# Where the softmax sums are added, and when finished units are written back, in a two-layer graph kernel on one core

## The chip, the cores and the metric

The kernel runs on one core of one Trainium2 chip. The core has five engines with instruction streams of their own: TensorE (PE in the profile) for matrix products and transposes, VectorE (DVE), ScalarE (ACT), GpSimd (POOL) and SyncE (SP), which here starts most transfers. TensorE writes its results to PSUM, a small memory from which VectorE and ScalarE read. The metric is the device time of one execution in microseconds (us), as the median of several runs.

## The reference

Two layers, each followed by a residual sum and a layer norm. The first is a graph convolution with batch norm, the second a masked attention with 4 heads of 64 over 2048 nodes, for each of 8 batches of 256 features. The change touches the second alone.

```python
# layer 0: x is (8, 2048, 256), adj is (2048, 2048)
x = _layernorm(x + _L0_gnn_ref(x, adj, W1, b1, g1, be1, W2, b2, g2, be2))
# layer 1
qkv = h @ W                                   # W: (256, 768)
q, k, v = ...                                 # 4 heads of 64
mask = jnp.where(adj == 0, -jnp.inf, 0.0)
scores = jnp.einsum('bhid,bhjd->bhij', q, k) / np.sqrt(HEAD_DIM) + mask
attn = jax.nn.softmax(scores, axis=-1)
out = jnp.einsum('bhij,bhjd->bhid', attn, v)  # heads side by side: (8, 2048, 256)
x = _layernorm(x + out)
```

## The kernel before

Layer 0 ends at about 1510 us of the profiled span. The attention then works on 64 units, one for each batch (8), pair of heads (HP = 2) and block of 512 query columns (NCH = 4), so 8 units to a batch. A unit has 16 steps, one for each tile of 128 keys. Scores of both heads are computed transposed (keys on partitions), masked by adding a large negative number, raised to the exponential without subtracting a maximum, multiplied by v, and divided by their sum at the end. (A second path with maxima runs only if a sum leaves a safe range.)

One step, in the four functions that every step calls:

```python
def scores(g):                     # PE: "S" in the prediction
    st = ps_s.tile([P, 2, CH], F32, name="st")          # ps_s: 2 buffers
    for h in range(2):
        hs = slice(h * HD, (h + 1) * HD)
        for r in range(2):
            nc.tensor.matmul(st[r * HD : (r + 1) * HD, h, :],
                kt[hs, j * P + r * HD : j * P + (r + 1) * HD], qt[hs, cols], start=True, stop=True)

def mask_scores(g, st):            # DVE
    p = probs[g] = ap_.tile([P, 2, CH], F32, name="prob", bufs=13)
    nc.vector.scalar_tensor_tensor(p, mask[...], MASKED, st, op0=ALU.mult, op1=ALU.add)

def exps(g):                       # ACT
    nc.scalar.activation(probs[g], probs[g], AF.Exp)

def weigh(g):                      # PE: "W"
    if j == 0:
        outs[u] = ps_o.tile([P, 2, CH], F32, name="out_ps")   # ps_o: 1 buffer
    ...                            # 4 matmuls into outs[u], summed over the 16 steps

def add_up(g):                     # GpSimd: sums over the key tiles
    if j == 1:
        accs[u] = ap_.tile([P, 2, CH], F32, name="acc")
        nc.gpsimd.tensor_add(accs[u], probs[g - 1], probs[g])
    elif 1 < j < NT - PE_SUM:      # PE_SUM = 3, NT = 16: 12 adds to a unit
        nc.gpsimd.tensor_add(accs[u], accs[u], probs[g])
```

What follows when a unit is done. All small PSUM tiles are called `pm` and share a pool of two buffers (`ps_m`, bufs=2): those of the sums, of the transposes and of the projections.

```python
def finish_out(u):                 # in step 15, right behind weigh
    ots[u] = ap_.tile([P, CH], F32, name="ot")
    nc.scalar.copy(ots[u], outs[u][:, 0, :])
    nc.vector.tensor_add(ots[u], outs.pop(u)[:, 1, :], ots[u])

def finish_sums(u):                # PE: the last PE_SUM tiles and acc, over partitions
    pm = ps_m.tile([P, BR], F32, name="pm")
    parts = [probs.pop(g) for g in range((u + 1) * NT - PE_SUM, (u + 1) * NT)]
    parts.append(accs.pop(u))
    for n, part in enumerate(parts):
        for h in range(2):
            for q in range(2):
                nc.tensor.matmul(pm[...], ones[:, :32], part[:, h, q * BR : (q + 1) * BR],
                                 start=(n == 0), stop=(n == len(parts) - 1))
    ...
    nc.scalar.copy(sts[u], pm)     # the tile "sm"

def finish_turn_sums(u):           # PE: 2 transposes; DVE: copy out, reciprocal
    pq = ps_m.tile([P, 2, P], F32, name="pm")
    for i in range(2):
        nc.tensor.transpose(pq[:, i, :], sm[:, i * P : (i + 1) * P], ident)
    nc.vector.tensor_copy(sums_all[:, u]..., pq...)
    nc.vector.reciprocal(sts[u], sums_all[:, u])

def finish_turn(u):                # PE: 4 transposes of "ot"
    pm = pms[u] = ps_m.tile([P, TPC, P], F32, name="pm")
    for i in range(TPC):
        nc.tensor.transpose(pm[:, i, :], ot[:, i * P : (i + 1) * P], ident)

def finish(u, half):               # DVE: 4 small products added to x1
    ...
```

Beside this, each batch's input is prepared while the batch before it is worked on, by functions of `Layer1Input`: `load` (DMA), `bn` (ACT), `norm` (PE transposes; DVE sum and layer norm statistics), `root` (GpSimd, four small instructions), `apply` (ACT), `turn` (PE transposes of x1 into `pm`, ACT copies them out) and `project` (PE products for q, k or v into `pm`; ACT or DVE copies them out). Finished rows get their last layer norm by `emit_stats` (DVE), `root` and `emit` (ACT, then DMA out).

```python
def apply(self, b, c, half):       # ACT: 2 instructions on x1
    self.ln[b, c].apply(range(IT * half, IT * (half + 1)))

def turn(self, b, c, half):
    pm = self.psum.tile([P, ND, BR], F32, name="pm")
    ...                            # 4 transposes
    nc.scalar.copy(self.x1t[b][:, :, r0 : r0 + BR], pm)

def emit_stats(self, b, c):
    ln = self.ln[b, c] = LayerNorm(self.pool, self.x1[b, c])
    ln.stats(range(TPC))           # 4 BN_STATS, 4 aggregates
```

All that stands beside the steps is put into a table by unit and step, and the order of the loop is the order of the instructions on PE, DVE, ACT and GpSimd:

```python
LEAD = 3
for u in range(NU - 1):
    b, hp, c = units[u]
    at_step(u + 1, 0, finish_sums, u)
    at_step(u + 1, 3, finish_turn_sums, u)
    at_step(u + 1, 3, finish_turn, u)
    at_step(u + 1, 3, finish, u, 0)
    at_step(u + 1, 4, finish, u, 1)
    if hp == HP - 1:
        j = 6 if c == 2 else 12
        at_step(u + 1, j, inp.emit_stats, b, c)
        at_step(u + 1, j + 2, inp.root, b, c)
        for half in range(2):
            at_step(u + 1, j + 5 + half, inp.emit, b, c, half)
# (cut: the table of the next batch's input; it is in the diff)

for g in range(NU * NT):
    u, j = divmod(g, NT)
    ahead = g + LEAD < NU * NT
    if ahead:
        st = scores(g + LEAD)
    if j == NT - 1:
        weigh(g)
        finish_out(u)
    if ahead:
        mask_scores(g + LEAD, st)
        exps(g + LEAD)
    for f, args in side.get((u, j), ()):
        f(*args)
    if j < NT - 1:
        weigh(g)
    add_up(g)
```

Of the kernel before, what the change touches and what calls it, by code (L numbers as in the profile page):

```python
# [26 lines left out]
def tile_gcn_then_masked_attention(  # L27
# [22 lines left out]
    NT = N // P  # L50
# [4 lines left out]
    NCH = N // CH  # L55
    TPC = CH // P
# [186 lines left out]
    IT = BR // P  # L243
    NU = B * HP * NCH
# [37 lines left out]
    class Layer1Input:  # L282
# [54 lines left out]
            r0 = c * CH + half * BR  # L337
            nc.scalar.copy(self.x1t[b][:, :, r0 : r0 + BR], pm)  # L338

        def emit_stats(self, b, c):  # L340
            ln = self.ln[b, c] = LayerNorm(self.pool, self.x1[b, c])
            ln.stats(range(TPC))

        def emit(self, b, c, half):
            self.apply(b, c, half)
# [46 lines left out]
    def attention():  # L392


        with tc.tile_pool(name="attn", bufs=2) as ap_, tc.tile_pool(
# [4 lines left out]
            inp = Layer1Input(ap_, ps_m, NCH + 3)  # L400
            units = [(b, hp, c) for b in range(B) for hp in range(HP) for c in range(NCH)]
            probs, accs, outs, ots, sts, pms = {}, {}, {}, {}, {}, {}

            PE_SUM = 3

            def scores(g):
                u, j = divmod(g, NT)
# [15 lines left out]
            def mask_scores(g, st):  # L423
                j, cols = g % NT, units[g // NT][2] * CH
                cols = slice(cols, cols + CH)
                p = probs[g] = ap_.tile([P, 2, CH], F32, name="prob", bufs=13)
                nc.vector.scalar_tensor_tensor(  # L427
                    p, mask[:, j, cols][:, None, :].to_broadcast([P, 2, CH]), MASKED, st,
                    op0=ALU.mult, op1=ALU.add,
                )  # L430

            def exps(g):
                nc.scalar.activation(probs[g], probs[g], AF.Exp)  # L433
# [16 lines left out]
            def add_up(g):  # L450
                u, j = divmod(g, NT)
                if j == 1:
                    accs[u] = ap_.tile([P, 2, CH], F32, name="acc")
                    nc.gpsimd.tensor_add(accs[u], probs[g - 1], probs[g])  # L454
                elif 1 < j < NT - PE_SUM:
                    nc.gpsimd.tensor_add(accs[u], accs[u], probs[g])  # L456

            def finish_out(u):
# [4 lines left out]
            def finish_sums(u):  # L463

                pm = ps_m.tile([P, BR], F32, name="pm")
                parts = [probs.pop(g) for g in range((u + 1) * NT - PE_SUM, (u + 1) * NT)]
                parts.append(accs.pop(u))
                for n, part in enumerate(parts):
                    for h in range(2):
                        for q in range(2):  # L470
                            r0 = 32 * (2 * h + q)
                            nc.tensor.matmul(  # L472
                                pm[r0 : r0 + 32, :], ones[:, :32],
                                part[:, h, q * BR : (q + 1) * BR],
                                start=(n == 0), stop=(n == len(parts) - 1),
                            )
                for g in range(u * NT, (u + 1) * NT - PE_SUM):
                    del probs[g]
                sts[u] = ap_.tile([P, BR], F32, name="sm")
                nc.scalar.copy(sts[u], pm)  # L480

            def finish_turn_sums(u):
                sm = sts.pop(u)
# [4 lines that stand above are left out]
                nc.vector.tensor_copy(  # L488
                    sums_all[:, u].rearrange("p (q i) h -> p i h q", q=2),
                    pq.rearrange("p i (h q r) -> p i h q r", h=2, q=2)[:, :, :, :, 0],  # L490
                )
                sts[u] = ap_.tile([P, TPC, 2], F32, name="ri")
                nc.vector.reciprocal(sts[u], sums_all[:, u])

            def finish_turn(u):
                pm = pms[u] = ps_m.tile([P, TPC, P], F32, name="pm")
                ot = ots.pop(u)
                for i in range(TPC):
                    nc.tensor.transpose(pm[:, i, :], ot[:, i * P : (i + 1) * P], ident)  # L499

            def finish(u, half):
                b, hp, c = units[u]
                for i in range(IT * half, IT * (half + 1)):
                    t = inp.x1[b, c][:, i, :]
                    for h in range(2):
                        z = t[:, hp * P + h * HD : hp * P + (h + 1) * HD]
                        nc.vector.scalar_tensor_tensor(
                            z, pms[u][:, i, h * HD : (h + 1) * HD], sts[u][:, i, h : h + 1], z,
                            op0=ALU.mult, op1=ALU.add,
                        )  # L510
# [4 lines left out]
            side = {}  # L515

            def at_step(u, j, f, *args):
                u, j = u + j // NT, j % NT
                side.setdefault((u, j), []).append((f, args))

            per_b = HP * NCH
            for u in range(NU - 1):
                b, hp, c = units[u]
                at_step(u + 1, 0, finish_sums, u)
                at_step(u + 1, 3, finish_turn_sums, u)
                at_step(u + 1, 3, finish_turn, u)
                at_step(u + 1, 3, finish, u, 0)
                at_step(u + 1, 4, finish, u, 1)
                if hp == HP - 1:
                    j = 6 if c == 2 else 12  # L530
                    at_step(u + 1, j, inp.emit_stats, b, c)
                    at_step(u + 1, j + 2, inp.root, b, c)
                    for half in range(2):
                        at_step(u + 1, j + 5 + half, inp.emit, b, c, half)
            for b in range(B):
                u0 = b * per_b
                for c in range(NCH):

                    for n, w in enumerate((1, 2, 0)):
                        at_step(u0 + c, (6, 9, 12)[n], inp.project, b, 1, c, w)  # L540
                    if b + 1 == B:
                        continue

                    late = 3 * (c == NCH - 1)
                    u = u0 + 3 + c
                    at_step(u - 1, 15 + late, inp.load, b + 1, c)
                    at_step(u, 2 + late, inp.bn, b + 1, c)
                    for half in range(2):
                        at_step(u, 6 + 3 * half + late, inp.norm, b + 1, c, half)
                    at_step(u, 11 + late, inp.root, b + 1, c)  # L550
                    for half in range(2):
                        at_step(u, 13 + half + (4 if late else 0), inp.apply, b + 1, c, half)
                    for half in range(2):
                        at_step(u + 1, 4 if late else 1, inp.turn, b + 1, c, half)
                    for n, w in enumerate((1, 2, 0)):
                        at_step(u + 1, (8, 10, 13)[n] if late else (6, 9, 12)[n],
                                inp.project, b + 1, 0, c, w)

            for c in range(NCH):
                inp.load(0, c)  # L560
# [11 lines left out]
            with tc.manual_schedule(engines=IN_ORDER):  # L572
                for g in range(LEAD):
                    mask_scores(g, scores(g))
                    exps(g)
# [13 lines that stand above are left out]
                    if j < NT - 1:  # L589
                        weigh(g)  # L590
                    add_up(g)
                u = NU - 1
                b, _, c = units[u]
                finish_sums(u)
                finish_turn_sums(u)
                finish_turn(u)
                for half in range(2):
                    finish(u, half)
                inp.emit_stats(b, c)
                inp.root(b, c)  # L600
                for half in range(2):
                    inp.emit(b, c, half)

    def attention_with_maxima():

        with tc.tile_pool(name="full", bufs=2) as ap_, tc.tile_pool(
# [8 lines left out]
            inp = Layer1Input(ap_, ps_m, NCH)  # L615
            for b in range(B):
# [51 lines left out]
                                z, po, sm, z, op0=ALU.mult, op1=ALU.add  # L668
                            )
                for c in range(NCH):  # L670
                    inp.emit_stats(b, c)
                    inp.root(b, c)
                    for half in range(2):
                        inp.emit(b, c, half)
# [66 lines left out]
```

## Time and profile before

| | before |
|---|---|
| median time | 4025.23 us (4021.12 to 4027.15, 3 runs) |
| span of the profiled run | 4024.4 us |
| PE busy | 3814.2 us, 95% |
| POOL busy | 1965.4 us, 49% (before the attention it does next to nothing) |
| DVE busy | 1938.5 us, 48% |
| ACT busy | 1634.9 us, 41% |
| one GpSimd add of 128x1024 | 2365 ns |
| one DVE mask of 128x1024 | 1219 ns |
| one ACT exponential of 128x1024 | 1056 ns |
| granted PE clock, 1600 to 3990 us | 1.00 |

The shares are those of the whole span. The attention takes the last 2500 us or so, and what the change is worth is read there. In the views of the profile each line has a start in us from the span's start, a duration, an engine, a line of the kernel, the operation, what it writes and reads, and how many instructions are put together; a bracket tells how long the engine sat idle before it, and what ended that. The matmuls of PE are pipelined, so their starts tell more than their durations. A wait line has the engine, the line and tile that waited, what it waited for, and then us in total, times, and the longest wait. One matmul of the program in this number format stands as two records in the profile.

### The profile page before, as it was taken

How to read it: one execution, taken by the hardware profiler on the slowest of the kernel's cores; microseconds unless marked ns; L12 is line 12 of the kernel's file. 1: busy time of each engine (PE TensorE's matmuls, PEld its weight loads, DVE VectorE, ACT ScalarE, POOL GpSimd, SP SyncE). 2: the span in 40 equal slices, each digit the busy share in tenths (PEclk: the TensorE clock that was granted, in tenths of full speed). 3: DMA queues.
4: the chain of work that ended last, by engine and by line, in shares of the span. 5: the costliest groups of instructions: out<-in, count | busy, mean ns of one | idle time of the engine just before them, and what ended most of it. 6: DMA issues, size and time to landing. Idle time of an engine off the chain costs nothing.

```text
span 4024.4 us, 57339 instructions
## 1 busy us (share of the span) xinstructions
PE 3814.2 (95%) x24226; PEld 1580.8 (39%) x24226; DVE 1938.5 (48%) x2874; ACT 1634.9 (41%) x2005; POOL 1965.4 (49%) x1103
## 2 busy tenths in 40 slices
PE   3599999999997998999999999999999999999997
PEld 3244444444443443333333333333333333333332
DVE  6411111111112443666666666666666666666665
ACT  6000000000001434555555556556555555555554
POOL 0000000000000003778778777777787877877887
PEclk7799999999998998999999999999999999999998
DMA  5110110111003761001001001001001001000000
GB/s 209 65 53 29 45 52 34 50 53 52 32 31 131 233 205 64 5 13 38 12 17 38 12 17 38 12 17 38 12 12 43 12 12 43 12 12 24 10 1 23
DMA packets 77229, 181.80 MB, mean 45 GB/s; under 512 B 6176, under 2 KB 55840, under 8 KB 66592
## 3 DMA queue, kind: packets, MB, share of 16 engines
q1 hardware_dynamic: 67600, 123.49, 9.3%
q0 software_dynamic: 9360, 54.53, 3.3%
q8 instruction: 192, 3.15, 0.3%
q14 instruction: 77, 0.63, 0.1%
HBM read 106.70 MB, written 71.30 MB: 44 GB/s over the span
## 4 chain that ended last, share of the span: by engine, by line
PE 86%; ACT 4%; DVE 3%; issue 1%; POOL 1%; DMA 1%; SPq 0%; ACTq 0%; DVEq 0%; POOLq 0%
PE pa L183 22%; PE out_ps L445 20%; PE st L415 19%; PE pm L363 6%; PE py L229 6%; PE ph L195 5%; PE pm L375 3%; ACT prob L433 2%; ACT x L277 2%; PE pm L472 2%; DVE prob L427 2%; POOL acc L456 1%; PE pm L312 1%; PE pm L499 1%; PE pm L332 1%
## 5 line engine op out<-in xcount | busy, mean ns | idle before, releaser
L456 POOL TENSOR_TENSOR acc<-acc,prob 128x1024 f32<-128x1024 f32 x704 | 1664.9, 2365 | 168.5 <-ACT prob L433 120.6
L427 DVE SCALAR_TENSOR_TENSOR prob<-mask,st 128x1024 f32<-128x1024 uint8 x1024 | 1241.8, 1219 | 648.6 <-PE st L415 640.3
L433 ACT ACTIVATE prob<-prob 128x1024 f32<-128x1024 f32 x1024 | 1080.5, 1056 | 1049.1 <-DVE prob L427 1041.3
L445 PE MATMUL out_ps<-prob,v 64*64 64x512 f32 x8192 | 1089.1, 598 | 0.1
L415 PE MATMUL st<-qt,kt 64*64 64x512 f32 x8192 | 1074.3, 590 | 0.9 <-DVE prob L427 0.9
L183 PE MATMUL pa<-at,xb 128*128 128x512 f32 x2048 | 886.1, 593 | 47.0 <-DMA xb<-in_x_dram 47.0
L183 PEld LDWEIGHTS pa<-at,xb 128*128 128x128 f32 x2048 | 389.8, 190 | 537.7 <-issue 537.7
L204 POOL DMA_DIRECT2D h_d<-h x32 | 17.3, 540 | 1151.3 <-ACT h L202 1151.3
L415 PEld LDWEIGHTS st<-qt,kt 64*64 64x64 f32 x8192 | 313.4, 133 | 567.5 <-issue 505.3
L202 ACT ACTIVATE h<-ph,b1s 128x512 f32<-128x512 f32 x128 | 87.9, 687 | 1066.0 <-PE ph L195 1066.0
L445 PEld LDWEIGHTS out_ps<-prob,v 64*64 64x64 f32 x8192 | 281.6, 132 | 508.7 <-issue 438.7
L190 DVE COPY ag<-pa 128x512 f32<-128x512 f32 x64 | 44.2, 691 | 823.7 <-PE pa L183 823.7
L454 POOL TENSOR_TENSOR acc<-prob 128x1024 f32<-128x1024 f32 x64 | 152.0, 2375 | 284.1 <-ACT prob L433 284.1
L363 PE MATMUL pm<-x1t,wq 128*128 128x512 f32 x512 | 254.8, 622 | 0.9 <-ACT x1t L338 0.9
L229 PE MATMUL py<-hin,w2s 128*128 128x512 f32 x512 | 222.6, 598 | 21.4 <-ACT hin L222 21.4
L195 PE MATMUL ph<-ag,w1s 128*128 128x512 f32 x512 | 231.1, 599 | 0.0
L203 DVE BATCH_NORM_STATS2 st<-h 128x6 f32<-128x512 f32 x128 | 88.9, 694 | 157.1 <-ACT h L202 157.1
L229 PEld LDWEIGHTS py<-hin,w2s 128*128 128x128 f32 x512 | 98.1, 192 | 145.8 <-issue 114.0
L363 PEld LDWEIGHTS pm<-x1t,wq 128*128 128x128 f32 x512 | 88.1, 191 | 160.3 <-issue 150.9
L222 ACT ACTIVATE hin<-hin,sh,sc 128x512 f32<-128x512 f32 x128 | 93.4, 801 | 138.1 <-DMA hin<-h_d 138.1
L195 PEld LDWEIGHTS ph<-ag,w1s 128*128 128x128 f32 x512 | 94.6, 190 | 131.3 <-issue 107.2
L277 ACT ACTIVATE x<-x,ln_nm,ln_rs 128x256 f32<-128x256 f32 x256 | 136.1, 585 | 24.2 <-POOL ln_nm L273 24.2
(83 smaller groups left out, 1815.3 us busy)
## 6 DMA issues: line engine op xcount, KB each, us to landing
h_d<-h POOLq DMA_DIRECT2D x32, 1024.0 KB, 4.1
hin<-h_d SPq DMA_DIRECT2D x32, 1024.0 KB, 5.9
a<-in_adj_dram SPq DMA_DIRECT2D x16, 1024.0 KB, 7.1
xb<-in_x_dram SPq DMA_DIRECT2D x8, 2048.0 KB, 8.1
y_d<-y POOLq DMA_DIRECT2D x32, 512.0 KB, 6.1
yt<-y_d SPq DMA_DIRECT2D x32, 512.0 KB, 3.2
x<-in_x_dram SPq DMA_DIRECT2D x32, 512.0 KB, 3.9
out_dram<-x SPq DMA_DIRECT2D x32, 512.0 KB, 2.9
```

Source lines behind the costliest of these rows:

```text
L183: nc.tensor.matmul(pa, xb[:, m, d * P : (d + 1) * P], at[:, m, c * CH : (c + 1) * CH], start=(m == 0), stop=(m == NT - 1),)
L195: nc.tensor.matmul(ph, w1s[:, d, f * P : (f + 1) * P], ag[:, d, :], start=(d == 0), stop=(d == ND - 1),)
L229: nc.tensor.matmul(py, w2s[:, f, o * P : (o + 1) * P], h[:, f, :], start=(f == 0), stop=(f == NH - 1),)
L277: nc.scalar.activation(self.t[:, i, :], self.t[:, i, :], AF.Identity, bias=self.nm[:, i : i + 1], scale=self.rs[:, i : i + 1],)
L363: nc.tensor.matmul(pm, wq[:, d, wcols], xt[:, d, cols], start=(d == 0), stop=(d == ND - 1))
L375: nc.tensor.matmul(pm[:, j * P : (j + 1) * P], xt[:, d, t * P : (t + 1) * P], wq[:, d, wcols], start=(d == 0), stop=(d == ND - 1),)
L415: nc.tensor.matmul(st[r * HD : (r + 1) * HD, h, :], kt[hs, j * P + r * HD : j * P + (r + 1) * HD], qt[hs, cols], start=True, stop=True,)
L427: nc.vector.scalar_tensor_tensor(p, mask[:, j, cols][:, None, :].to_broadcast([P, 2, CH]), MASKED, st, op0=ALU.mult, op1=ALU.add,)
L433: nc.scalar.activation(probs[g], probs[g], AF.Exp)
L445: nc.tensor.matmul(outs[u][hs, r, :], inp.qkv[b, hp][2][rs, j, hs], probs[g][rs, h, :], start=(j == 0), stop=(j == NT - 1),)
L454: nc.gpsimd.tensor_add(accs[u], probs[g - 1], probs[g])
L456: nc.gpsimd.tensor_add(accs[u], accs[u], probs[g])
```

## The change

The change does four things to the attention. It adds 15 of 16 probability tiles on GpSimd where it was 13, so that TensorE sums one tile and the accumulator; in the last four units, where the queue of projections has ended, TensorE sums four. It moves `finish_sums` from step 0 to step 4 of the next unit, which gives GpSimd time to end its adds. It moves the finishing transposes from step 3 to step 6, beside the first projection, so that fewer places interrupt the run of scores and products. And it lays the transposes of x1 (`turn`) at step 2, apart from the sums, with `apply` at steps 0 and 1; before, they stood at step 1 (in each batch's last block at step 4). The schedule becomes the same for all blocks: the final statistics come in two halves at steps 13 and 15, their root and `emit` early in the unit after, the projections in the order q, k, v at steps 6, 9 and 12, and the end of the kernel runs through the same table.

```diff
@@ Layer1Input
-        def emit_stats(self, b, c):
-            ln = self.ln[b, c] = LayerNorm(self.pool, self.x1[b, c])
-            ln.stats(range(TPC))
+        def emit_stats(self, b, c, half):
+            if half == 0:
+                self.ln[b, c] = LayerNorm(self.pool, self.x1[b, c])
+            self.ln[b, c].stats(range(IT * half, IT * (half + 1)))
@@ attention
-            PE_SUM = 3
+            def on_pe(u):
+
+                return 4 if u >= NU - NCH else 1
@@ add_up
-                elif 1 < j < NT - PE_SUM:
+                elif 1 < j < NT - on_pe(u):
                     nc.gpsimd.tensor_add(accs[u], accs[u], probs[g])
@@ finish_sums (its three uses of PE_SUM become on_pe(u))
@@ the table
-            for u in range(NU - 1):
+            for u in range(NU):
                 b, hp, c = units[u]
-                at_step(u + 1, 0, finish_sums, u)
-                at_step(u + 1, 3, finish_turn_sums, u)
-                at_step(u + 1, 3, finish_turn, u)
-                at_step(u + 1, 3, finish, u, 0)
-                at_step(u + 1, 4, finish, u, 1)
+                at_step(u + 1, 4, finish_sums, u)
+                at_step(u + 1, 6, finish_turn_sums, u)
+                at_step(u + 1, 6, finish_turn, u)
+                at_step(u + 1, 6, finish, u, 0)
+                at_step(u + 1, 7, finish, u, 1)
                 if hp == HP - 1:
-                    j = 6 if c == 2 else 12
-                    at_step(u + 1, j, inp.emit_stats, b, c)
-                    at_step(u + 1, j + 2, inp.root, b, c)
                     for half in range(2):
-                        at_step(u + 1, j + 5 + half, inp.emit, b, c, half)
+                        at_step(u + 1, 13 + 2 * half, inp.emit_stats, b, c, half)
+                        at_step(u + 2, 2 + half, inp.emit, b, c, half)
+                    at_step(u + 2, 0, inp.root, b, c)
             for b in range(B):
                 u0 = b * per_b
                 for c in range(NCH):
 
-                    for n, w in enumerate((1, 2, 0)):
-                        at_step(u0 + c, (6, 9, 12)[n], inp.project, b, 1, c, w)
+                    for w in range(3):
+                        at_step(u0 + c, 6 + 3 * w, inp.project, b, 1, c, w)
                     if b + 1 == B:
                         continue
 
-                    late = 3 * (c == NCH - 1)
                     u = u0 + 3 + c
-                    at_step(u - 1, 15 + late, inp.load, b + 1, c)
-                    at_step(u, 2 + late, inp.bn, b + 1, c)
+                    at_step(u, 4, inp.load, b + 1, c)
+                    at_step(u, 8, inp.bn, b + 1, c)
+                    at_step(u, 14, inp.root, b + 1, c)
                     for half in range(2):
-                        at_step(u, 6 + 3 * half + late, inp.norm, b + 1, c, half)
-                    at_step(u, 11 + late, inp.root, b + 1, c)
-                    for half in range(2):
-                        at_step(u, 13 + half + (4 if late else 0), inp.apply, b + 1, c, half)
-                    for half in range(2):
-                        at_step(u + 1, 4 if late else 1, inp.turn, b + 1, c, half)
-                    for n, w in enumerate((1, 2, 0)):
-                        at_step(u + 1, (8, 10, 13)[n] if late else (6, 9, 12)[n],
-                                inp.project, b + 1, 0, c, w)
+                        at_step(u, 9 + 3 * half, inp.norm, b + 1, c, half)
+                        at_step(u + 1, half, inp.apply, b + 1, c, half)
+                        at_step(u + 1, 2, inp.turn, b + 1, c, half)
+                    for w in range(3):
+                        at_step(u + 1, 6 + 3 * w, inp.project, b + 1, 0, c, w)
@@ the end of the kernel
-                u = NU - 1
-                ...                     # the same finishing calls, one after another
+                for u in (NU, NU + 1):
+                    for j in range(NT):
+                        for f, args in side.get((u, j), ()):
+                            f(*args)
```

More of the change, by code (lines that the diff above doesn't have):

```diff
@@ L465, in finish_sums @@
                 pm = ps_m.tile([P, BR], F32, name="pm")
-                parts = [probs.pop(g) for g in range((u + 1) * NT - PE_SUM, (u + 1) * NT)]
+                parts = [probs.pop(g) for g in range((u + 1) * NT - on_pe(u), (u + 1) * NT)]
                 parts.append(accs.pop(u))
@@ L476, in finish_sums @@
                             )
-                for g in range(u * NT, (u + 1) * NT - PE_SUM):
+                for g in range(u * NT, (u + 1) * NT - on_pe(u)):
                     del probs[g]
@@ L591, in attention @@
                     add_up(g)
-                u = NU - 1
[L593 to L602, printed above, removed]
+                for u in (NU, NU + 1):
+                    for j in range(NT):
+                        for f, args in side.get((u, j), ()):
+                            f(*args)
     def attention_with_maxima():
@@ L670, in attention_with_maxima @@
                 for c in range(NCH):
-                    inp.emit_stats(b, c)
+                    for half in range(2):
+                        inp.emit_stats(b, c, half)
                     inp.root(b, c)
```

## The prediction

> **What bounds the kernel now.** I read, in this order: the page's busy shares and groups, the waits of TensorE (PE), and the instructions in order of time around one boundary between units. S below is one step's scores (L415), W its weighing (L445), W15 the last W of a unit, W0 the first of the next. The page puts the busiest helper, GpSimd, at:
>
> ```profile
> L456 POOL TENSOR_TENSOR acc<-acc,prob 128x1024 f32<-128x1024 f32 x704 | 1664.9, 2365 | 168.5 <-ACT prob L433 120.6
> ```
>
> One add costs 2.37 us, and 12 of them per unit 28.4 us. A batch of 8 units takes 307 us (the same PE pattern recurs at 1852.6, 2159.7, 2466.8), a unit 38.4 us, so GpSimd is not the bound. PE is: from 1600 to 2520 us it is busy 907.75 of 920 us. What little it waits in the attention is x1's transposes (L332):
>
> ```profile
> PE pm L332 <- ACT sm L480: 16.8, 21, 0.9
> PE pm L332 <- ACT prob L433: 11.9, 7, 1.7
> ```
>
> These 29 us are waits for one of the two `pm` buffers. PE's order, read as distances between starts:
>
> ```profile
> 1992.62 1.04 PE L415 MATMUL st<-qt,kt 64*64 64x512 f32 x8
> 1993.59 1.50 PE L472 MATMUL pm<-prob,ones 128*32 128x256 f32 x24
> 1994.91 0.61 PE L472 MATMUL pm<-acc,ones 128*32 128x256 f32 x8
> ...
> 1996.36 1.04 PE L415 MATMUL st<-qt,kt 64*64 64x512 f32 x8
> ...
> 1999.79 1.04 PE L415 MATMUL st<-qt,kt 64*64 64x512 f32 x8
> 2000.76 0.44 PE L486 MATMUL pm<-ident,sm 128*128 128x128 f32 x2
> ...
> 2002.48 1.04 PE L415 MATMUL st<-qt,kt 64*64 64x512 f32 x8
> ...
> 2005.91 1.04 PE L415 MATMUL st<-qt,kt 64*64 64x512 f32 x8
> 2006.88 0.66 PE L312 MATMUL pm<-ident,yt 128*128 128x128 f32 x4
> ...
> 2010.10 1.04 PE L415 MATMUL st<-qt,kt 64*64 64x512 f32 x8
> ...
> 2021.22 1.04 PE L415 MATMUL st<-qt,kt 64*64 64x512 f32 x8
> ...
> 2025.01 1.04 PE L415 MATMUL st<-qt,kt 64*64 64x512 f32 x8
> ```
>
> Elsewhere in this answer S to S is 1.72 us: one S and one W of 0.86 each. Anything above that is what stands between: the sums 3.74 - 1.72 = 2.02 us; the six finishing transposes alone 0.97; a projection with four transposes beside it 2.47; the same projection alone (2021.22 to 2025.01) 2.07. The 24 sum records of the three probability tiles start 1.32/24 = 0.055 us apart.
>
> Then a boundary between units, all engines. Look at what runs while the sums (L472) hold PE:
>
> ```profile
> 2148.77 1.04 PE L445 MATMUL out_ps<-prob,v 64*64 64x512 f32 x8
> 2149.63 1.04 PE L415 MATMUL st<-qt,kt 64*64 64x512 f32 x8
> 2149.88 0.58 ACT L460 COPY ot<-out_ps 128x512 f32<-128x512 f32 x1 [0.19 <-PE out_ps L445]
> 2150.50 0.69 DVE L461 TENSOR_TENSOR ot<-out_ps,ot 128x512 f32<-128x512 f32 x1 [1.90 <-ACT ot L460]
> 2150.60 1.50 PE L472 MATMUL pm<-prob,ones 128*32 128x256 f32 x24
> 2151.11 2.34 DVE L427 SCALAR_TENSOR_TENSOR prob<-mask,st 128x1024 f32<-128x1024 uint8 x2
> 2152.47 1.09 PE L445 MATMUL out_ps<-prob,v 64*64 64x512 f32 x8
> ```
>
> W15 starts at 2148.77. ACT copies half of its result, DVE adds the other half and is done at 2151.19, 2.42 us after W15's start; only then is the single `out_ps` buffer free for W0. PE doesn't notice, because the sums are in between: W0 comes at 2152.47 anyway.
>
> [...]
>
> **What the change removes from PE.** (1) In 60 of 64 units two of three probability tiles are no longer summed on PE: 16 records of 0.055 us = 0.88 us, 53 us in all; the last four units sum one tile more (0.44 us each), net 51. (2) The six finishing transposes go beside the projection at step 6. Four transposes beside a projection cost 2.47 - 2.07 = 0.40, so six 0.60, instead of 0.97 alone: 0.37 us in 59 units, 22. (3) The waits of 29 us at L332 go. Sum: 102 us less.
>
> **What it moves into PE's way.** The built program's order of instructions and its waits show three new places.
>
> (a) *The boundary.* With the sums at step 4, W0 stands directly behind W15 and one S, 1.72 us after W15's start, but `out_ps` is free only after 2.42, with 0.05 for the signal 2.47: 0.75 us lost. The next S needs the score buffer whose mask runs from 2.34 to 3.56, where PE would come at 3.35: 0.25 more. Together 1.0 us. Behind the units in which layer norm statistics now stand at steps 13 and 15 (30 of 63 boundaries), it is more. Two BN_STATS and two aggregates are about 1.1 us of DVE. Those at step 13 push mask, exponential and so the copy back by 0.38; those at step 15 stand between two masks, so the second ends at 6.2 instead of 4.7, and the S after the next, due at 5.7, waits 0.5: 1.9 us in all. 33 x 1.0 + 30 x 1.9 = 90 us.
>
> (b) *x1's transposes.* They now stand at step 2, and their two applies (ACT, 1.08 us a pair) at steps 0 and 1. After W15 at 0: the exponentials of the last step and of step 0 end at 4.66 and 5.8, the first apply at 6.9, the next exponential at 7.95, the second apply at 9.05. PE reaches the transposes at 6.3 (S at 5.3, and 0.97). The first half waits 0.65 us and the second, after half a microsecond of transposes, 1.65: 2.3 us. Behind a boundary with statistics the same count gives 2.85. Of 28 such places half are of each kind: 14 x 2.3 + 14 x 2.85 = 72 us. So the old wait of 0.8 (a buffer) is replaced by a longer one (data).
>
> (c) *Step 6.* Sum transposes, output transposes and projection take three `pm` tiles one after another, and there are two buffers. The projection must wait until DVE has copied the sums out, and that copy stands behind the step's mask. The view of before shows the same pair at step 3, where the S had started at 1999.79 and the mask at 2000.97:
>
> ```profile
> 2002.11 0.17 DVE L488 COPY sums_all<-pm 128x8 f32<-128x8 f32 x1
> ```
>
> Its end is 2.49 us after S, 2.55 with the signal. PE wants the projection at 0.97 + 0.70 = 1.67: 0.88 us lost, 59 times, 52 us.
>
> Sum of the new waits: 90 + 72 + 52 = 214 us. Balance: 4025 - 102 + 214 = 4137; the end of the kernel, where PE now waits 4.27 us for GpSimd's accumulator, may give 2 or 3 back. I say 4135.
>
> **GpSimd.** 14 adds are 33.1 us; one set of root instructions is 1.9 (2105.20 to 2107.14), and one unit in eight has two sets: 36.9 at most, against 38.4 of PE before and more after. It is nearly full, and waits for the statistics of step 15, some 5 us into the unit, but the sums need its result only at step 4 of the next unit, about 10 us after W15. I count nothing.
>
> **The rivals.** *PE's work alone decides*: the three waits hide somewhere and the 102 us come through, 3925 us. For it: PE is 98.7% busy, so work removed counts. Against it: PE has nothing to do in a wait, as its order is fixed, and each of the three is a chain longer than the PE work beside it. *GpSimd becomes the bound*: its in-order adds fall behind through the roots, and PE waits at the sums on top; that would give about 1 us in the fuller units, 4150 or more. For it: 33.1 + 1.9 leaves little room. Against: four steps of slack. *Only the firm waits count*: the W0 buffer (0.75 x 63 = 47) and step 6 (52) come, but ACT gets its applies done earlier than my count, and the statistics hide; 4025 - 102 + 99 = 4022, no change. For it: GpSimd's roots are early enough, and a stall at one place gives ACT and DVE time for the next. Against: at step 2 ACT has two exponentials and two applies in 4.4 us between its copy's end and the transposes, with the first mask not done before 3.56.
>
> **Range and chances.** The lower edge takes the firm waits and half of the rest, (214 - 99)/2 = 58: 4080, less 20 for gains that I put too low, 4060. The upper edge adds 50 us for GpSimd and for restarts after each wait (some 0.1 us at 180 places is 18): 4185. The 2% line is at 4106, under my figure by 29 us; slower by over 2% 0.66, within 2% 0.27, faster 0.07, for the rival in which the waits hide.
>
> **What would show it.** PE waits that were not there: at W0 for DVE's add of `ot`, near 0.75 us in each of 63 boundaries; at the transposes of x1 for ACT's applies, over 1 us; at the projection of step 6 for DVE's copy of the sums, 0.9. PE's busy time should fall by some 70 us, while the span grows. GpSimd's busy time should rise by about 60 x 2 - 4 = 116 adds of 2.37, 275 us. If PE waits at the sums for GpSimd, or the three waits are missing, I am wrong; if the waits are there but short, only my sizes are.

## The result, and the profile after

| | before | after |
|---|---|---|
| median time, runs side by side | 4023.45 us | 4166.64 us |
| ratio | | 1.036, 95% interval 1.0342 to 1.0378 |
| PE busy | 3814.2 us, 95% | 3844.5 us, 92% |
| POOL busy | 1965.4 us | 2235.7 us |
| DVE, ACT busy | 1938.5, 1634.9 us | 1942.2, 1642.8 us |

The changed kernel is 143 us slower; 4135 was predicted. TensorE has fewer records (23298 instead of 24226), yet it isn't done sooner. The lines of the page that answer to those shown of before are these; in the groups the first number behind the bar is busy time, then the mean in ns, then the idle time just before and what ended it:

```profile
L459 POOL TENSOR_TENSOR acc<-acc,prob 128x1024 f32<-128x1024 f32 x820 | 1937.5, 2363 | 162.1 <-ACT prob L436 105.7
L448 PE MATMUL out_ps<-prob,v 64*64 64x512 f32 x8192 | 1105.4, 606 | 36.1 <-DVE ot L464 36.1
L364 PE MATMUL pm<-x1t,wq 128*128 128x512 f32 x512 | 254.9, 622 | 41.8 <-DVE sums_all L491 40.9
```

GpSimd does 116 adds more (820 + 64 against 704 + 64), each as fast as before. On PE two groups now have idle time ahead of them that they did not have. PE's waits from 1600 to 4130 us (us in total, times, longest):

```profile
PE pm L364 <- DVE sums_all L491: 40.9, 59, 1.0
PE pm L332 <- ACT x L277: 38.9, 84, 0.9
PE out_ps L448 <- DVE ot L464: 36.1, 63, 0.6
PE pm L312 <- ACT yt L301: 22.1, 35, 1.7
PE st L418 <- DVE prob L430: 0.4, 1, 0.4
```

Before, this list held the buffer waits of L332 and little else. The first three new lines are the three places of the prediction; the fourth, L312, is not in it. GpSimd is absent.

These waits understate what is lost: the boundary below has 0.57 us of wait at W0, but its scores come 1.02 us late. What a place really costs is read from the distance between the starts of two neighbouring groups of scores: 1.716 us when nothing stands between. All that is over it, summed by step over a batch of 8 units (means of the six middle batches):

| step | 0 | 1 | 2 | 3 | 4 | 6 | 8 | 9 | 10 | 12 | 13 | batch |
|---|---|---|---|---|---|---|---|---|---|---|---|---|
| before | 16.2 | 6.6 | 0 | 7.7 | 3.1 | 15.8 | 2.1 | 16.7 | 2.1 | 15.0 | 2.1 | 87.5 |
| after | 8.2 | 1.4 | 15.7 | 2.4 | 9.3 | 29.2 | 0 | 22.5 | 0 | 18.8 | 0 | 107.4 |

Over the whole attention the rest is 695.0 us before and 840.7 after: 146 us more, which is the loss (the start and the end of the kernel give 5 back). Now each place in the order of time. First a boundary between units (start, duration, engine, line, what it does):

```profile
2462.15 1.04 PE L448 MATMUL out_ps<-prob,v 64*64 64x512 f32 x8
2463.01 1.04 PE L418 MATMUL st<-qt,kt 64*64 64x512 f32 x8
2463.25 0.59 ACT L463 COPY ot<-out_ps 128x512 f32<-128x512 f32 x1
2463.87 0.69 DVE L464 TENSOR_TENSOR ot<-out_ps,ot 128x512 f32<-128x512 f32 x1 [1.69 <-ACT ot L463]
2464.48 1.21 DVE L430 SCALAR_TENSOR_TENSOR prob<-mask,st 128x1024 f32<-128x1024 uint8 x1
2464.62 1.09 PE L448 MATMUL out_ps<-prob,v 64*64 64x512 f32 x8 [0.57 <-DVE ot L464]
2465.74 1.09 PE L418 MATMUL st<-qt,kt 64*64 64x512 f32 x8
```

The chain copy, add, W0 is the one shown of before, with the same offsets (2.41 us from W15's start to the add's end), but PE has nothing between S and W0. S to S is 2.73 us, 1.02 too long, in every one of 63 boundaries.

A few steps on come x1's transposes:

```profile
2469.68 0.33 PE L332 MATMUL pm<-ident,x 128*128 128x128 f32 x1 [0.49 <-ACT x L277]
2470.17 0.55 PE L332 MATMUL pm<-ident,x 128*128 128x128 f32 x3 [0.16 <-ACT x L277]
2470.97 1.08 ACT L277 ACTIVATE x<-x,ln_nm,ln_rs 128x256 f32<-128x256 f32 x2
2471.61 0.33 PE L332 MATMUL pm<-ident,x 128*128 128x128 f32 x1 [0.89 <-ACT x L277]
2472.10 0.65 PE L332 MATMUL pm<-ident,x 128*128 128x128 f32 x3 [0.17 <-ACT x L277]
2472.68 1.99 PE L448 MATMUL out_ps<-prob,v 64*64 64x512 f32 x8
2474.45 1.72 PE L418 MATMUL st<-qt,kt 64*64 64x512 f32 x8
2475.99 1.03 PE L448 MATMUL out_ps<-prob,v 64*64 64x512 f32 x8
```

PE waits for each apply in turn, as computed. The W behind them is held up with them: its exponentials had been done since 2466.78, and it starts at 2472.68, behind the last transpose. But look at the group behind: eight records that elsewhere take 0.86 us from start to start take 1.77, and the next 1.54. The busy times by stretch have the reason. Each line has the stretch, its length, five busy times with their numbers of instructions (PE, its weight loads, DVE, ACT, POOL), and then the granted PE clock, here 1.00 and 0.56:

```profile
2466.00:2472.00 6.00, 3.98 (x29) 1.10 (x21) 4.14 (x7) 4.71 (x8) 5.03 (x6) 1.00 0.00 1
2472.00:2475.50 3.50, 3.40 (x19) 1.31 (x23) 0.00 (x0) 2.93 (x6) 3.42 (x2) 0.56 0.02 5
```

The trace's clock records show why: PE's clock is granted at half for one window of 3.41 us, from 2472.41 us on. From 1600 us to the last steps there are 18 such windows, all at x1's transposes (they begin between 0.6 us before and 0.7 us after the last of these starts); 10 of the 28 places with these transposes have none. Before the change there was no such window.

Step 6, where the projection needs the buffer of the sums' transposes:

```profile
2481.44 1.04 PE L418 MATMUL st<-qt,kt 64*64 64x512 f32 x8
...
2482.61 1.22 DVE L430 SCALAR_TENSOR_TENSOR prob<-mask,st 128x1024 f32<-128x1024 uint8 x1 [0.49 <-PE st L418]
2482.68 0.60 PE L502 MATMUL pm<-ident,ot 128*128 128x128 f32 x4
2483.75 0.16 DVE L491 COPY sums_all<-pm 128x8 f32<-128x8 f32 x1
...
2483.97 1.98 PE L364 MATMUL pm<-x1t,wq 128*128 128x512 f32 x4 [0.69 <-DVE sums_all L491]
```

The copy ends 2.47 us after S started (2.49 in the view of before), and the projection starts at 2.53.

And step 9 in a batch's fourth unit, the place that I had not seen coming:

```profile
2357.83 1.04 PE L418 MATMUL st<-qt,kt 64*64 64x512 f32 x8
...
2359.70 1.51 ACT L301 ACTIVATE yt<-yt,sh,sc 128x512 f32<-128x512 f32 x2
2360.55 0.33 PE L312 MATMUL pm<-ident,yt 128*128 128x128 f32 x1 [1.68 <-ACT yt L301]
2361.11 1.04 ACT L436 ACTIVATE prob<-prob 128x1024 f32<-128x1024 f32 x1
2361.26 0.55 PE L312 MATMUL pm<-ident,yt 128*128 128x128 f32 x3 [0.38 <-ACT yt L301]
```

The batch norm of the next batch's rows (`bn`, ACT) stands at step 8, behind that step's exponential, and PE reads its result at step 9. The change had moved it there from step 2 (step 5 in a batch's last block), with its reader four steps behind.

### The profile page after: what moved, and what is told of

Same layout as the page of the kernel before. It is cut to its first block, busy times and chain, and to the rows that moved or that the text cites. A ratio compares the mean times of both kernels' runs of the same rounds, so it can differ in the third digit from the quotient of the medians.

```text
span 4165.2 us, 55719 instructions
## 1 busy us (share of the span) xinstructions
PE 3844.5 (92%) x23298; PEld 1548.6 (37%) x23298; DVE 1942.2 (47%) x2874; ACT 1642.8 (39%) x2005; POOL 2235.7 (54%) x1219
## 4 chain that ended last, share of the span: by engine, by line
PE 76%; DVE 11%; ACT 5%; issue 2%; POOL 2%; DMA 1%; DVEq 0%; SPq 0%; POOLq 0%; ACTq 0%
PE pa L183 21%; PE out_ps L448 17%; PE st L418 16%; DVE prob L430 8%; PE py L229 5%; PE ph L195 5%; PE pm L364 5%; PE pm L376 3%; ACT prob L436 2%; PE pm L475 2%; ACT x L277 1%; DVE ln_st L265 1%; POOL acc L459 1%; ACT yt L301 1%; DVE ot L464 1%
## 5 line engine op out<-in xcount | busy, mean ns | idle before, releaser
L459 POOL TENSOR_TENSOR acc<-acc,prob 128x1024 f32<-128x1024 f32 x820 | 1937.5, 2363 | 162.1 <-ACT prob L436 105.7
L448 PE MATMUL out_ps<-prob,v 64*64 64x512 f32 x8192 | 1105.4, 606 | 36.1 <-DVE ot L464 36.1
L418 PE MATMUL st<-qt,kt 64*64 64x512 f32 x8192 | 1092.1, 599 | 5.1 <-DVE prob L430 1.3
```

The source lines that it names most:

```text
L418: nc.tensor.matmul(st[r * HD : (r + 1) * HD, h, :], kt[hs, j * P + r * HD : j * P + (r + 1) * HD], qt[hs, cols], start=True, stop=True,)
L448: nc.tensor.matmul(outs[u][hs, r, :], inp.qkv[b, hp][2][rs, j, hs], probs[g][rs, h, :], start=(j == 0), stop=(j == NT - 1),)
```

## The experiments

Two theories stood against each other. Mine: PE waits at fixed places because the change took away the work that had covered a chain there, put a reader right behind its writer, or asked for three tiles of a pool of two. The rival: GpSimd with 15 of 16 tiles is now the bound. "Rest" below is what stands between the scores over the whole attention, as in the table (695.0 before, 840.7 after).

**Undoing and doing single parts.** The first run takes the kernel before and moves the sums alone, so that GpSimd's load stays as it was.

```diff
-at_step(u + 1, 0, finish_sums, u)
-at_step(u + 1, 3, finish_turn_sums, u)   # and finish_turn, finish half 0; half 1 at 4
+at_step(u + 1, 3, finish_sums, u)
+at_step(u + 1, 7, finish_turn_sums, u)   # and finish_turn, finish half 0; half 1 at 8
```

> The kernel before with one thing changed: the sums move from step 0 to step 3, their transposes from step 3 to step 7. The work on PE stays the same. If PE lacks work between a unit's last weighing and the next unit's first (my theory), a wait of 1.0 us comes up at each of 63 boundaries, +64 us; the waits of 29 us at x1's transposes go, as their buffers are no longer held by the sums: 4060 us. If the place of the sums is of no weight and only the buffers count, 3996 us. If it is GpSimd's load that made the changed kernel slower, nothing comes up here either, as GpSimd adds 13 of 16 as before: 3996 to 4025 us.

Measured 4083.86 us, ratio 1.0146 (1.0129 to 1.0163), rest 755.0. (In one of four blocks of a batch the last layer norm's statistics are taken here before the unit's output has been added to x1, so they leave it out; the amount of work is the same.) PE's two largest waits:

```profile
PE out_ps L445 <- DVE ot L461: 55.0, 63, 1.8
PE pm L332 <- ACT sm L480: 5.8, 7, 0.8
```

The wait at W0 is there with GpSimd's old load: 1.02 us in 42 boundaries, and 1.91 in the 21 where two applies at steps 13 and 14 make ACT late for its copy. The old waits at x1's transposes shrink by 26 us. I had not counted on ACT in those 21; they are 19 of the 24 us that came over the expectation. Moving the sums, and the finishing transposes behind them, costs 60 us by itself.

The second run takes the kernel before and changes the number of tiles alone (`PE_SUM` becomes `on_pe(u)`, the sums stay at step 0).

> The kernel before with one thing changed: 15 of 16 tiles are added on GpSimd (13 in the last four units), and the sums stay at step 0. If removed PE work counts fully and GpSimd keeps up, 52 us less: 3973 us. If GpSimd isn't done with its adds when PE comes to the sums (the reason for the later place), PE waits there for the accumulator: with 1 us of wait a unit 4035 us, with 2 us 4100 us. If GpSimd is the true bound of the changed kernel, over 4100 us.

Measured 3990.6 us, ratio 0.9923 (0.9907 to 0.994), rest 667.7: faster than before. Of PE's waits:

```profile
PE pm L332 <- ACT sm L482: 18.2, 21, 0.9
...
PE out_ps L447 <- DVE ot L463: 6.4, 14, 0.5
PE pm L474 <- POOL acc L458: 3.7, 7, 0.5
```

GpSimd is in time even at step 0: PE waits for its accumulator 3.7 us in the whole run. So the later place, which cost 60 us, was not needed. The gain is 33 us and not 52 mostly because the sums, now half as long, no longer cover the boundary where ACT is late: step 0 reads 1.16 us in most units, but 1.91 in 21, which is 16 us. Two half-speed windows behind x1's transposes take about 3 more.

The third run takes the changed kernel and gives GpSimd 13 of 16 again (`return 3`).

> The changed kernel with one thing undone: GpSimd adds 13 of 16 tiles again, PE sums three and the accumulator, in all units. My theory: PE gets back 0.87 us in 60 units and loses 0.44 in four, and the waits stay: 4217 us. If GpSimd's load is what holds the changed kernel up, the time falls, below 4166 us.

Measured 4225.95 us, ratio to before 1.0501 (1.0483 to 1.0518), rest 895.8. All four waits stay as they were, and the step of the sums rises from 1.16 to 2.03 us. GpSimd's load isn't what holds the changed kernel up; the rival falls. (Of the 9 us over my figure about 5 are half-speed windows, 21 instead of 18: 14 behind x1's transposes and 7 at step 9.)

**Taking the waits away one by one**, each from the changed kernel.

```diff
 # e4: x1t is taken at the first turn instead of at load, and
-at_step(u0 + c, 6 + 3 * w, inp.project, b, 1, c, w)          # v (w = 2) at step 12
+at_step(u0 + c, (6, 9, 16)[w], inp.project, b, 1, c, w)      # v at step 0 of the next unit
 # the same for the projections of b + 1
```

> The changed kernel with the projection of v moved from step 12 to step 0 of the unit after, so that PE has 2.1 us of work between the last weighing and the first (x1's transposed tile is taken later, at the first transpose). No work is added. My theory: the wait at the first weighing (36 us idle on PE, and with what follows it about 1.02 us in each of 63 boundaries) goes in 59 places, -60 us, and x1's transposes wait some 0.5 us less in 28 places: 4092 us. If the boundary's chain is only a sign of engines that are late anyway, the wait comes up at the next step and the time stays at 4150 to 4166 us.

Measured 4080.78 us, ratio to before 1.0141 (1.0124 to 1.0157), rest 755.5, 85 less. Steps 0 and 12 together fall from 3.16 to 2.14 us; the wait at W0 is 1.7 us in all instead of 36. The chain at the boundary is hidden as soon as PE has 2.1 us of work there. The surplus over the expected 74 comes mostly from fewer half-speed windows (10).

```diff
 # e5
-at_step(u, 8, inp.bn, b + 1, c)
+at_step(u, 6, inp.bn, b + 1, c)
```

> The changed kernel with the batch norm of the next batch's rows (two ACT instructions, 1.5 us) at step 6 instead of step 8, so that it isn't one step ahead of the transposes that read it. The transposes of step 9 then find it done: step 9 falls from 4.81 to 2.54 us in one unit of eight and from 3.09 to 2.58 in three, 3.9 us a batch, 27 us in seven batches: 4139 us. If ACT is only short of time there, the wait moves to another of its outputs and the time stays within 5 us of 4166.

Measured 4138.13 us, ratio to before 1.0282 (1.0265 to 1.03), rest 809.9. Step 9 reads 2.47 and 2.51 us, and L312 is gone from PE's waits. The fourth wait is the cost of that placement, 28 us.

```diff
 # e6: finish_turn_sums, finish_turn, finish half 0 from step 6 to 7; half 1 from 7 to 8
-at_step(u + 1, 6, finish_turn_sums, u)
+at_step(u + 1, 7, finish_turn_sums, u)
```

> The changed kernel with the six finishing transposes at step 7 by themselves, as before the change, instead of beside the projection of step 6. By the buffer theory the projection no longer waits for the copy of the sums: step 6 falls from 3.64 to 2.08 us and step 7 rises from 0 to 0.97, 0.6 us less in 59 units, 35 us: 4131 us. If the wait had another cause (VectorE late with its mask), it stays and the lost merging comes on top: 4188 us.

Measured 4119.43 us, ratio to before 1.0237 (1.022 to 1.0254), rest 790.1. Step 6 reads 2.08 and step 7 0.97 us, 3.05 together against 3.64; the wait for L491 is gone. That is the 35 us; the other 12 come again with fewer windows (12) and a somewhat shorter step 9. Laying the transposes beside the projection was meant to save 0.37 us a unit and lost 0.6.

```diff
 # e7
-at_step(u + 1, 2, inp.turn, b + 1, c, half)
+at_step(u + 1, 3, inp.turn, b + 1, c, half)
```

> The changed kernel with x1's transposes at step 3 instead of step 2, one step further from the layer norm that feeds them. My theory: the waits there, 1.65 us in half of 28 units and 2.3 us in the others, shrink by 1.2 to 1.7 us each (40 us), and with the shorter pause the half-speed clock windows (18 of 3.41 us, about 1.7 us lost in each) go too, 30 us more: 4096 us. If the clock windows don't hang on this pause, 4126 us. If ACT is late by as much one step on, 4166 us.

Measured 4132.84 us, ratio to before 1.027 (1.0253 to 1.0287), rest 805.1: 34 us less, half of what I expected. Of PE's waits:

```profile
PE pm L475 <- ACT x1t L338: 26.7, 14, 1.9
PE pm L312 <- ACT yt L301: 22.2, 35, 1.7
PE pm L332 <- ACT x L277: 2.3, 14, 0.2
```

The wait for the applies is gone (38.9 to 2.3), but in 14 units one of 1.9 us comes up a step later: the sums need a `pm` buffer that ACT has not yet emptied, since in those units it also applies the last layer norm. And 8 windows remain; none stands directly behind x1's transposes any longer, 6 stand at step 9 and 2 behind the new wait. So the windows went where the pauses went.

**All four together**, by place alone: v at step 0, q and k at steps 9 and 12, `bn` at 6, x1's transposes at 3, sums at 5, finishing transposes at 7 and 8.

> The changed kernel with all four waits taken away at once by place alone: v's projection at step 0 of the next unit, batch norm at step 6, x1's transposes at step 3 and the sums at step 5 behind them, the finishing transposes alone at step 7, projections of q and k at steps 9 and 12 beside the next batch's transposes. No work is added or left out. If the four waits (with the half-speed clock windows that follow them) are the whole loss, what stands between the steps is content alone: 8 x (2.14 + 1.16 + 0.97 + 2.08 + 2.08) + 4 x (1.33 + 0.43 + 0.43) = 76.2 us a batch against 107.4 in the changed kernel, 234 us less: 3932 us, faster than before. If GpSimd with 15 of 16 tiles is a bound of its own, waits for its accumulator or for its free buffers come up in their place and the time stays over 3990 us.

Measured 3951.59 us, ratio to before 0.9816 (0.98 to 0.9833), rest 624.4, 77.2 us a batch against 76.2 computed. PE's waits from 1600 to 3930 us:

```profile
PE pm L489 <- ACT sm L483: 3.7, 1, 3.7
PE pm L475 <- ACT x1t L338: 2.6, 14, 0.2
PE pm L332 <- ACT x L277: 2.4, 15, 0.2
PE out_ps L448 <- DVE ot L464: 1.7, 3, 0.6
PE pm L475 <- POOL acc L459: 0.7, 1, 0.7
```

Its boundary shows v's projection (L376) in the place where before the change the sums stood:

```profile
2383.85 1.04 PE L448 MATMUL out_ps<-prob,v 64*64 64x512 f32 x8
...
2384.96 0.59 ACT L463 COPY ot<-out_ps 128x512 f32<-128x512 f32 x1
2385.57 0.69 DVE L464 TENSOR_TENSOR ot<-out_ps,ot 128x512 f32<-128x512 f32 x1 [1.63 <-ACT ot L463]
2385.68 2.05 PE L376 MATMUL pm<-wq,x1t 128*128 128x128 f32 x16
...
2387.66 1.09 PE L448 MATMUL out_ps<-prob,v 64*64 64x512 f32 x8
```

The add ends at 2386.26, W0 starts at 2387.66 without a wait. There is no half-speed window left between 1600 us and the end of the steps. With the same 15 of 16 tiles on GpSimd this version beats both kernels, the changed one by 215 us and the one before by 76. One by one the four moves gave 86, 28, 47 and 34 us, 195 in all, so little is left for a fifth cause.

A second version starts from the kernel before, takes the 15 of 16, leaves the sums at step 0 behind v's projection, and puts x1's transposes at step 2 (5 in the last block) and the finishing ones at step 4.

> A version that keeps what the runs show to pay. From the kernel before: 15 of 16 tiles on GpSimd, sums still at step 0, but behind the projection of v, which moves there from step 9; x1's transposes at step 2 (step 5 in a batch's last block), the finishing transposes alone at step 4. Against before: sums 52 us less, one interruption of the PE stream less in 59 units (some 0.2 us, 12 us), the waits at x1's transposes (29 us) gone, and the boundary's chain hidden behind 3.1 us of PE work: 3932 us. If GpSimd can't follow, PE waits at the sums and the time stays near 3990, that of the run with 15 of 16 alone.

Measured 3963.38 us, ratio to before 0.9848 (0.9832 to 0.9864), rest 635.6, 79.5 us a batch: better than before and than the tiles alone, 31 us over my figure. In a batch's last two units the old exceptions remain: x1's transposes there wait for VectorE (12.0 us in 7 waits), with a half-speed window behind three of the seven, and one norm stands alone.

## Why the prediction was right, and where its sizes were off

The direction, the range (4060 to 4185) and three of the four causes held; the sum was about 31 us too low. That it came so near is partly luck: (a) and the waits of (b) were counted 26 us too high together, and the two terms that were missing make 57.

| term of the sum | predicted | measured | read from |
|---|---|---|---|
| sums off PE | -51 | -51 | steps of the sums: 127.9 to 77.0 us |
| transposes beside a projection | -22 | -22 | 0.97 alone, 59 times; the 0.60 beside is the estimate |
| old waits at L332 gone | -29 | -35 | the steps of L332: 67.9 us, less 28 x 1.19 |
| (a) boundary | +90 | +75 | 63 x 1.02, and 10.5 at step 1 |
| (b) x1's transposes, waits | +72 | +61 | 14 x (3.05 - 1.19) + 14 x (3.69 - 1.19) |
| (b) half-speed windows behind them | 0 | +30 | 18 x 1.65 |
| (c) step 6 | +52 | +57 | 59 x (3.65 - 2.08 - 0.60) |
| norm behind `bn`, step 9 | 0 | +27 | 99.2 us less 72.0 with before's content |
| sum | +112 | +142 | |

The 1.19 us for eight transposes without a wait is from the two last versions. The 1.65 us are what a place with a window takes longer than a like one without (for example 4.74 against 3.05 us over steps 2 and 3).

(a) The firm part was exact: 0.75 + 0.25 predicted, 1.02 measured. The part for the statistics was too big, 1.9 where 1.3 came out. I let the statistics of step 13 push ACT's copy by 0.38; in the trace neighbouring VectorE operations overlap by about 0.1 us each (at the boundary of 2462.15 the aggregates of step 13 end at 2461.06 and the next mask starts at 2460.98), and the copy starts 1.10 us after W15 there too. Only the mask behind the second half is late, by 0.4.

(b) The order of the engines was as worked out, the waits 1.86 and 2.5 us instead of 2.3 and 2.85. What failed for the windows is the allowance "for restarts after each wait (some 0.1 us at 180 places is 18)", which I put into the upper edge alone. The 0.1 us was an estimate; before the change the 28 places at L332 cost 34.6 us for 28.7 us of waits, 0.2 us more for each. After 18 of these pauses PE ran at half clock for a whole window, 3.41 us.

(c) The step was right, 0.97 instead of 0.88 us: three `pm` tiles in one step, two buffers. The wait takes back more than the merging saves.

The missing term is the norm at step 9. I looked for what the change did to the waits of `pm`, `out_ps` and the applies, and did not follow `bn` from step 2 to step 8, where its reader is one step behind. The same look as for the applies would have shown it.

GpSimd: "I count nothing" held. It is 856 of 920 us busy in the mended version and PE waits for its accumulator once, 0.7 us. The rival "only the firm waits count" was right in part: the applies were done some 0.4 us earlier than counted and most of the statistics hid, but 61 of the 72 us at x1's transposes stayed, so it fell. "PE's work alone decides" fell too, though with all four waits removed the time comes near its figure (3951.59 against 3925).

The signs held but for one. The waits came at the three places, and GpSimd's busy time rose by 270 us, against 275 forecast. PE's busy time was to fall by some 70 us and rose by 30 (3814.2 to 3844.5). Half-speed work is busy for longer, about 30 us in the 18 windows (18 x 1.65). And a group of S or W is 1.04 us long in the views, while the next starts 0.86 us after it: back to back the last 0.18 us lies under the next group, at a pause it counts in full. As much at each of the 242 waits of the list would make 44 us, an estimate. So a change of PE's busy time isn't a change of its work.

## What to carry to other kernels

When an in-order engine is the bound, a piece of its side work can also cover somebody else's chain: before moving or shrinking one, measure the chain that runs beside it (here 2.4 us of copy and add against 1.72 us of other work), and leave something there that is as long. Go through every moved item with two questions: how many steps stand now between its writer and its reader, and how many tiles of its pool are open at once. A small schedule change can be checked in this way from the profile before it is run, and the parts of a change can then be kept apart: here one part was worth keeping (15 of 16), and the part that was to make it possible was not needed.

## What the runs showed of the hardware that I had not expected

A short pause cost more than its length here. In the changed kernel 1.86 or 2.5 us of waits around eight transposes were followed by a window of 3.41 us at half PE clock, about 1.65 us lost, at 18 of 28 places: 5 of the 14 with the shorter wait and 13 of the 14 with the longer. There were 12 such windows with the finishing transposes moved, 10 with v's projection moved, 8 with x1's transposes moved, and none with all waits gone. But a pause did not always bring one: in the last block of seven batches the kernel before has x1's transposes with a wait of 1.70 us that cost about 1.9 (3.07 us at step 4 instead of 1.19) and no window, while the same seven places had two with 15 of 16 tiles alone, and three in the last version.

The clock records of the changed kernel have all 18 at the same length, 3.413 us, and they start whole multiples of it apart (those at 2428.04 and 2472.41 us, for example, 13). Whether it matters how a pause falls into this grid was not shown. PE was not idle in the 3.41 us ahead of them: it was busy for 1.69 to 2.21 us.

Three stretches, each one window long, show that this busy time alone doesn't tell what follows. From 2424.62 to 2428.04 us of the changed kernel PE was busy 2.22 us, 1.75 of them with x1's transposes, and half clock followed. In the first run (sums at step 3) it was busy 1.60 us at a boundary, from 2986.46 to 2989.88, without any transpose, and full clock stayed. Nor does it take transposes: with x1's transposes at step 3, PE was busy 1.50 us from 2464.06 to 2467.47, with no transpose and one wait of 1.91, and half clock followed. What decides was not shown.
